# Order of all engines from a plan inside the program; the first gated state turned through DRAM

## The chip, the cores and the metric

The kernel runs on one core of a Trainium2 chip. A core has five engines that run side by side, each with a queue of its own that it works off in order: TensorE (matmuls and transposes into PSUM; PE in the profile, with its weight loads as PEld), VectorE (DVE), ScalarE (ACT), GpSimd (POOL) and SyncE (SP), which issues the DMAs here. The metric is the device time of the whole kernel in microseconds, median of three runs.

## The reference, cut to what matters

128 graphs of 128 nodes with 256 features each; every graph has its own 128x128 adjacency. Four layers, each added to x. Three are graph attention, the last a gated graph network of three steps:

```python
# layers 0, 1, 2 (attention), each with its own W and a
h = relu(layernorm(x))
Wh = h @ W
e = (Wh @ a1)[:, :, None] + (Wh @ a2)[:, None, :]
e = where(e > 0, e, 0.2 * e)
p = softmax(where(adj > 0, e, -9e15), axis=-1)
x = x + elu(p @ Wh)             # layer 2 also multiplies by nodemask
# layer 3 (gated): h = relu(layernorm(x)), then three times, i = 0, 1, 2
m = h @ weight[i]
ag = A.T @ m                    # A = (adj != 0)
r = sigmoid(ag @ w_ih[r].T + h @ w_hh[r].T + b)
z = sigmoid(ag @ w_ih[z].T + h @ w_hh[z].T + b)
n = tanh(ag @ w_ih[n].T + b_in + r * (h @ w_hh[n].T + b_hn))
h = (1 - z) * n + z * h
# out = x + h
```

All of it is in float32.

## The kernel before, in words

Graphs are taken four at a time: 32 groups, 512 columns (4 graphs x 128 nodes) in a PSUM bank. Two Python generators issue the work of a group: `gat(g)` the three attention layers and the start of the gated layer, `gru(g)` the three gated steps.

An attention layer (`attention`, L200) keeps nodes in partitions. `stats` (L170) takes mean and variance on VectorE and the reciprocal deviation rs on GpSimd (L182). ScalarE centres and clips into xn (L207). The two score vectors come from xn without forming Wh: the first on VectorE, one graph at a time (scr, L212), the second as a product pr on GpSimd (L217) that ScalarE scales and sums (L221). Four TensorE transposes (e, L229) turn the second score into a row. VectorE adds, masks and takes the maximum (L235 to L241), ScalarE the exponential (L245), TensorE transposes the probabilities (atp, L261), multiplies by xn (ahp, L272) and by W (hp, L285). ScalarE (L291) and VectorE (L293, L294) form elu and add it to xo, which GpSimd had prepared as x - 1 (L257). The next layer's statistics need xo, so one group's layers are a chain across all engines.

After the third layer the gated state hn (L317) is transposed to feature-major form by `turned` (L185): eight TensorE transposes into two banks (hTp, L191), copied out by ScalarE (L195) and VectorE (L197) into hT.

A gated step (`gru`, L324) works feature-major in two halves of 128 features. Four accumulators stand in four PSUM banks: nn, r, z (from the state and `whh`) and ni, with r, z and ni also fed from the aggregate ag and `wc` (L344; the products weight[i] @ w_ih are formed once in the setup). The state is turned back to node-major by TensorE (hnp, L335), copied by ScalarE (hn, L352), multiplied with the adjacency (agp, L361) and copied by VectorE (ag, L365). wn, r, n, z are activations on ScalarE (L385 to L402), the rest is VectorE (L392 to L408). The last state is turned back once more and added to x (o, L415), and the result is stored (L419).

PSUM's eight banks are split into three rings: two for attention ("gat"), four for the gates ("gru"), two for the turns ("tr"). Tiles come from pools with two buffers for most tags.

Order: the program's end (L428 to L434) issues `gat(0)`, `gat(1)`, then `gru(0)`, `gat(2)`, `gru(1)`, and so on, and the framework's own scheduler interleaves these streams into one order for each engine when the program is built. That order is fixed at run time: an engine whose next instruction waits does nothing else. The setup (weights, their transposes, wc) comes first. VectorE copies its PSUM results.

Of the kernel before, what the change touches and what calls it, by code (L numbers as in the profile page):

```python
# [17 lines left out]
EPS = 1e-5  # L18


@with_exitstack
def kernel(
# [23 lines left out]

    nc = tc.nc
# [3 lines left out]
    NG = B // G  # L51
    T = G * N
    STEPS = gweight.shape[0]
    assert N == P and B % G == 0 and B <= P and D == 2 * P and T == 512

    const = ctx.enter_context(tc.tile_pool(name="const", bufs=1))
    grp = ctx.enter_context(tc.tile_pool(name="grp", bufs=2))
    gw = ctx.enter_context(tc.tile_pool(name="gw", bufs=2))
    setup = ExitStack()
    su = setup.enter_context(tc.tile_pool(name="setup", bufs=2))  # L60
    psum = ctx.enter_context(tc.tile_pool(name="psum", bufs=1, space=bass.MemoryType.PSUM))
    BANKS = {"gat": 2, "gru": 4, "tr": 2}

    def bank(tag, name):
        return psum.tile([P, T], FT, tag=tag, name=name, bufs=BANKS[tag])

    def load(g):
        xt = grp.tile([P, G, D], FT, tag="x0", name=f"x_{g}")
        nc.sync.dma_start(xt, x[g * G : (g + 1) * G].rearrange("b n d -> n b d"))
        at = grp.tile([P, G, N], I32, tag="adj", name=f"adj_{g}")  # L70
        nc.sync.dma_start(at, adj[g * G : (g + 1) * G].rearrange("b i j -> i b j"))
        return xt, at

    loaded = {0: load(0)}


# [4 lines left out]

    W, VA = [], []
    for l, (w, a) in enumerate(((w0, a0), (w1, a1), (w2, a2))):
        wt = const.tile([P, KD, D], FT, name=f"w_{l}")
        nc.sync.dma_start(wt, w.rearrange("(k p) o -> p k o", p=P))
        ab = su.tile([P, 2, D], FT, tag="ab", name=f"ab_{l}")
        nc.sync.dma_start(ab, bass.AP(tensor=a.tensor, offset=a.offset, ap=[[0, P], [1, 2 * D]]))
        wa = su.tile([P, 2, KD], FT, tag="wa", name=f"wa_{l}")  # L90
        vp = bank("gat", f"vp_{l}")
        for s in range(2):
            for k in range(KD):
                scr = su.tile([P, D], FT, tag="scr", name=f"scr_{l}_{k}_{s}")
                nc.vector.scalar_tensor_tensor(
                    scr, wt[:, k, :], 1.0, ab[:, s, :], op0=OP.mult, op1=OP.mult,
                    accum_out=wa[:, s, k : k + 1],
                )
                c = s * KD + k
                nc.tensor.transpose(  # L100
                    vp[:, c * P : (c + 1) * P], wa[:, s, k : k + 1].to_broadcast([P, P]), ident
                )
        va = const.tile([P, 2, D], FT, name=f"va_{l}")
        nc.vector.tensor_copy(va.rearrange("p s d -> p (s d)"), vp)
        W.append(wt)
        VA.append(va)

    nm = su.tile([B, N], FT, tag="nm", name="nm")
    nc.sync.dma_start(nm, nodemask)
    nmp = bank("gat", "nmp")  # L110
    nc.tensor.transpose(nmp[:, :B], nm, ident[:B, :B])
    nmT = const.tile([P, B], FT, name="nmT")
    nc.vector.tensor_copy(nmT, nmp[:, :B])


    def transposed(src, dst, nm_):
        rows = src.shape[0] // P
        t = su.tile([P, rows, D], FT, tag="wld", name=f"{nm_}_ld")
        nc.sync.dma_start(t, src.rearrange("(r p) d -> p r d", p=P))
        for k in range(KD):  # L120
            for r0 in range(0, rows, 4):
                n = min(4, rows - r0)
                ps = bank("gat", f"{nm_}_{k}_{r0}")
                for r in range(n):
                    nc.tensor.transpose(
                        ps[:, r * P : (r + 1) * P], t[:, r0 + r, k * P : (k + 1) * P], ident
                    )
                nc.vector.tensor_copy(dst[:, k, r0 * P : (r0 + n) * P], ps[:, : n * P])
# [341 lines left out]
```

## Time and profile before

| | |
|---|---|
| time | 3127.16 us, median of 3 (3126.57 to 3129.3) |
| span of the profiled execution | 3125.1 us |
| TensorE busy | 2941.1 us, 94% |
| VectorE, ScalarE, GpSimd busy | 2163.8, 1349.4, 530.0 us |
| DMA | 48.03 MB, mean 15 GB/s |
| first gate product nn | at 121.09 us |
| stores of neighbouring results, middle groups | 94.27 us apart |

A busy row adds the times of an engine's instructions. Idle time in front of an instruction is put down to what released it last. Matmul ends are modelled and overlap their successors, so the distance of two starts says more of a matmul's cost than its printed length. A float32 matmul stands as two passes in the records, a transpose as one.

### The profile page before, as it was taken

Reading aid. Unit: us, or ns where it says so; the run is one execution under the profiler, and the core shown is the slowest. Engines: PE = TensorE matmul, PEld = TensorE weight load, DVE = VectorE, ACT = ScalarE, POOL = GpSimd, SP = SyncE. Lnnn points to the kernel's source line nnn. Section 1 sums busy time; section 2 is a strip of 40 time slices with the busy share of each in tenths; the row PEclk is TensorE's granted clock in tenths of the full one; section 3 lists DMA queues with packets and bytes.
Section 4 is the critical chain, followed back from the end, with each engine's and each line's share of the span. In section 5 each row is a group of like instructions: output and inputs, shape, how many; then the busy total and the mean of one; then the engine's idle time right before and its main releaser. Section 6 shows DMA issues by size and latency. Waiting matters only on the chain.

```text
span 3125.1 us, 32601 instructions
## 1 busy us (share of the span) xinstructions
PE 2941.1 (94%) x11105; PEld 1714.3 (55%) x11105; DVE 2163.8 (69%) x4731; ACT 1349.4 (43%) x3265; POOL 530.0 (17%) x454
## 2 busy tenths in 40 slices
PE   5699999999999999999999999999999999999999
PEld 3455555555555555555555555555555555555554
DVE  5667776767776777776777677677667677767663
ACT  1344444444444444444444444444444444444442
POOL 1212111212111212121112121112121121111110
PEclk8899999999999999999999999999999999999999
DMA  2000000000000000000000000000000000000000
GB/s 85 11 17 11 7 18 17 17 18 11 7 18 17 18 17 11 7 17 18 17 18 11 7 17 18 18 12 13 11 18 17 17 11 7 17 14 7 8 1 14
DMA packets 56199, 48.03 MB, mean 15 GB/s; under 512 B 3296, under 2 KB 55648, under 8 KB 56032
## 3 DMA queue, kind: packets, MB, share of 16 engines
q1 hardware_dynamic: 56032, 45.95, 4.6%
q8 instruction: 87, 1.43, 0.2%
q14 instruction: 80, 0.66, 0.1%
HBM read 29.17 MB, written 16.78 MB: 15 GB/s over the span
## 4 chain that ended last, share of the span: by engine, by line
PE 70%; DVE 13%; ACT 9%; POOL 6%; issue 1%; DMA 0%; ACTq 0%; SPq 0%; POOLq 0%; DVEq 0%
PE r L344 15%; PE z L344 15%; PE ni L344 9%; PE hp L285 7%; PE nn L344 7%; PE ahp L272 6%; POOL pr L217 5%; ACT xn L207 4%; PE agp L361 3%; DVE st L175 3%; DVE xo L294 3%; DVE xo L293 3%; ACT pr L221 2%; PE hnp L335 2%; PE e L229 2%; PE atp L261 2%
## 5 line engine op out<-in xcount | busy, mean ns | idle before, releaser
L212 DVE SCALAR_TENSOR_TENSOR scr<-xn,rs,va 128x256 f32<-128x256 f32 x384 | 386.0, 1053 | 73.0 <-POOL rs L182 71.1
L344 PE MATMUL r<-ag,wc 128*128 128x512 f32 x768 | 372.1, 593 | 0.0
L344 PE MATMUL ni<-ag,wc 128*128 128x512 f32 x768 | 371.4, 592 | 0.0
L285 PE MATMUL hp<-w,ah 128*128 128x256 f32 x1536 | 368.3, 383 | 0.7 <-DVE ah L279 0.7
L344 PE MATMUL z<-ag,wc 128*128 128x512 f32 x768 | 361.4, 592 | 0.0
L257 POOL TENSOR_SCALAR xo<-xo 128x1024 f32<-128x1024 f32 x64 | 67.5, 1055 | 1596.4 <-DVE mv L176 1596.4
L285 PEld LDWEIGHTS hp<-w,ah 128*128 128x128 f32 x1536 | 284.2, 190 | 76.8 <-DVE ah L279 26.3
L293 DVE SCALAR_TENSOR_TENSOR xo<-hp,xo 128x512 f32<-128x512 f32 x192 | 131.0, 683 | 253.6 <-ACT t L291 253.6
L221 ACT ACTIVATE pr<-pr,rs 128x256 f32<-128x256 f32 x384 | 190.4, 496 | 183.5 <-POOL pr L217 183.5
L291 ACT ACTIVATE t<-hp 128x512 f32<-128x512 f32 x192 | 114.7, 597 | 353.5 <-PE hp L285 353.5
L344 PE MATMUL nn<-h,whh 128*128 128x512 f32 x512 | 261.8, 593 | 0.0
L344 PE MATMUL z<-h,whh 128*128 128x512 f32 x512 | 261.5, 592 | 0.0
L344 PE MATMUL r<-h,whh 128*128 128x512 f32 x512 | 261.5, 592 | 0.0
L392 DVE SCALAR_TENSOR_TENSOR n<-r,wn 128x512 f32<-128x512 f32 x192 | 131.4, 685 | 185.2 <-ACT r L390 185.2
L217 POOL TENSOR_TENSOR pr<-xn,va 128x1024 f32<-128x1024 f32 x96 | 236.2, 2461 | 96.6 <-ACT xn L207 96.6
L245 ACT ACTIVATE pe<-em,nmx 128x128 f32<-128x128 f32 x384 | 148.8, 389 | 209.3 <-DVE nmx L241 209.3
L361 PEld LDWEIGHTS agp<-am,hn 128*128 128x128 f32 x1536 | 204.5, 192 | 61.3 <-issue 61.0
L344 PEld LDWEIGHTS z<-ag,wc 128*128 128x128 f32 x768 | 143.3, 190 | 167.5 <-issue 167.4
L397 ACT ACTIVATE n<-n,bi 128x512 f32<-128x512 f32 x192 | 138.3, 720 | 213.1 <-DVE n L396 210.5
L390 ACT ACTIVATE r<-r,brz 128x512 f32<-128x512 f32 x192 | 131.3, 684 | 215.1 <-PE r L344 215.0
L344 PEld LDWEIGHTS ni<-ag,wc 128*128 128x128 f32 x768 | 143.5, 190 | 142.7 <-issue 132.2
L361 PE MATMUL agp<-am,hn 128*128 128x128 f32 x1536 | 218.2, 275 | 0.0
(91 smaller groups left out, 4636.6 us busy)
## 6 DMA issues: line engine op xcount, KB each, us to landing
x<-in_x_dram SPq DMA_DIRECT2D x32, 512.0 KB, 3.9
out_dram<-o SPq DMA_DIRECT2D x32, 512.0 KB, 2.9
adj<-in_adj_dram SPq DMA_DIRECT2D x32, 256.0 KB, 2.7
w<-in_L_gnn_W_dram SPq DMA_DIRECT2D x3, 256.0 KB, 6.9
ab<-in_L_gnn_a_dram SPq DMA_DIRECT2D x3, 256.0 KB, 6.6
whh_ld<-in_L_gnn_w_hh_dram SPq DMA_DIRECT2D x1, 768.0 KB, 8.4
wih_ld<-in_L_gnn_w_ih_dram SPq DMA_DIRECT2D x1, 768.0 KB, 5.9
gt_ld<-in_L_gnn_weight_dram SPq DMA_DIRECT2D x3, 256.0 KB, 2.6
```

The costliest lines, as they stand in the source:

```text
L212: nc.vector.scalar_tensor_tensor(scr, xn[:, b, :], rs[:, b : b + 1], VA[l][:, 0, :], op0=OP.mult, op1=OP.mult, accum_out=e[:, 0, b : b + 1],)
L217: nc.gpsimd.tensor_tensor(pr, xn, VA[l][:, 1 : 2, :].to_broadcast([P, G, D]), op=OP.mult)
L221: nc.scalar.activation(pr[:, b, :], pr[:, b, :], AF.Copy, scale=rs[:, b : b + 1], accum_out=e[:, 1, b : b + 1],)
L245: nc.scalar.activation(pe[:, b, :], em[:, b, :], AF.Exp, bias=nmx[:, b : b + 1], accum_out=sm[:, b : b + 1])
L272: nc.tensor.matmul(ps[:, c * P : (c + 1) * P], xn[:, c, k * P : (k + 1) * P], at[:, c * P : (c + 1) * P], start=True, stop=True,)
L285: nc.tensor.matmul(hp[:, b * D : (b + 1) * D], ah[:, k, c * P : (c + 1) * P], W[l][:, k, :], start=(k == 0), stop=(k == KD - 1),)
L293: nc.vector.scalar_tensor_tensor(u, hp, 0.0, u, op0=OP.max, op1=OP.add)
L344: nc.tensor.matmul(ps, w[:, k, c * P : (c + 1) * P], v[k], start=start, stop=stop)
L361: nc.tensor.matmul(ps[:, b * P : (b + 1) * P], hn[k][b], am[:, b, :], start=True, stop=True)
L390: nc.scalar.activation(r, pr, AF.Tanh, bias=brz[:, cr : cr + 1], scale=0.5)
L392: nc.vector.scalar_tensor_tensor(n, r, 1.0, wn, op0=OP.add, op1=OP.mult)
L397: nc.scalar.activation(n, n, AF.Tanh, bias=bi[:, cn : cn + 1])
```

## The change

The kernel's arithmetic stays. What changes is who sets the order, and how the first gated state is turned.

1. A plan in the program. No instruction is issued directly any more. Each is handed to `plan.add` with its engine, an estimated cost, a rank and the values that it reads and writes. `Plan.issue` then plays the program through with these costs: at each step it takes the engine that can start earliest, and of its instructions that could start within 0.1 us of the first the one of lowest rank. An instruction may run ahead of the lowest unfinished rank by at most 6. The list that comes out is issued with the framework's scheduler switched off (`manual_schedule`), so it is each engine's order.
2. Tiles by first use. A value takes its buffer in a ring when its first instruction is placed, so the order of buffers follows the plan; `takes` makes the first instruction of a chain claim what the rest needs.
3. Ranks. Group g's gated step i has 3g + i, its attention layer l has 3g - 7.5 + 2l. The layers of a group lie thus over the gated steps of groups up to two earlier, and two groups' layers overlap. ScalarE's and VectorE's gate work is put forward by 2 (URGENT).
4. Groups. The first and the last have two graphs, the 31 between them four.
5. The first gated state. VectorE transposes 32x32 blocks of hn into tr, one DMA stores tr to DRAM, four load it back with the blocks exchanged (hT). Its blocks lie so that the first gated step reads the state with a strided view (`first`): runs of 32 values. The eight TensorE transposes and two copies of `turned` are gone.
6. Small moves: setup copies go from VectorE to ScalarE; the exponential and the normalised probabilities are written in place of the scores (em); GpSimd's xo comes ahead of the score transposes in the program; gate products are ranked rather than listed.

The core of the diff:

```diff
+class Plan:
+    LAG = {"PE": 0.26, "DVE": 0.08, "ACT": 0.08, "POOL": 0.12, "SP": 2.4}
+    WINDOW = 0.1
+    AHEAD = 6.0
...
+        def choose(engine):
+            found = [(start(op), op) for op in ready[engine]]
+            found = [f for f in found if f[0] is not None]
+            if not found:
+                return None
+            first = min(t for t, _ in found)
+            soon = [(op.rank, t, i) for i, (t, op) in enumerate(found) if t <= first + self.WINDOW]
+            _, t, i = min(soon)
+            return t, found[i][1]
...
+        for op in order:
+            for v in op.vals:
+                v.t
+            op.fn()
...
-    NG = B // G
+    SIZES = [2] + [G] * ((B - 4) // G) + [2]
+    NG = len(SIZES)
...
+    def dve(cols):
+        return 0.1 + cols / 960
+
+    def act(cols):
+        return 0.25 + cols / 1400
+
+    def pool(cols):
+        return 0.35 + cols / 512
...
+        rank = 3.0 * g - LEAD + 2.0 * l
...
-        hT = turned(hn, grp, "h0", f"{g}_3")
...
+        def blocks(k):
+            add("DVE", dve(n * P), rank, lambda: nc.vector.transpose(
+                tr.t[:, :, :F].rearrange("p j (k b c) -> p k b j c", k=KD, b=n)[:, k],
+                hn.t[:, :, k * P : (k + 1) * P].rearrange("p b (j r) -> p b j r", j=Q),
+            ), reads=[hn], writes=[(tr, k)])
...
+        add("SP", 0.45, rank, lambda: nc.sync.dma_start(
+            d.t.rearrange("q r j f -> (q r) j f"), tr.t[:, :, :F]), reads=[tr], writes=[d])
+
+        def back(j):
+            add("SP", 0.45, rank, lambda: nc.sync.dma_start(
+                hT.t[j * 32 : (j + 1) * 32, :, :F], d.t[:, :, j, :].rearrange("q r f -> r q f")
+            ), reads=[d], writes=[(hT, j)])
...
+        def first(k):
+
+            t = h0.t[:, :, :F].rearrange("p q (k b c) -> p k b q c", k=KD, b=n_g)
+            return t[:, k]
...
-    AHEAD = 2
-    for g in range(min(AHEAD, NG)):
-        run(gat(g))
-    for g in range(NG):
-        run(gru(g))
-        if g + AHEAD < NG:
-            run(gat(g + AHEAD))
+    LEAD, URGENT = 7.5, 2.0
+    for g in range(NG):
+        gru(g, *gat(g))
+    with tc.manual_schedule():
+        plan.issue()
```

## The prediction

> **What bounds the kernel now.** I read the busy shares first, then TensorE's own waits, then one steady wait and the start in the time-ordered view.
>
> ```profile
> PE 2941.1 (94%) x11105; PEld 1714.3 (55%) x11105; DVE 2163.8 (69%) x4731; ACT 1349.4 (43%) x3265; POOL 530.0 (17%) x454
> ...
> PE   5699999999999999999999999999999999999999
> ...
> PEclk8899999999999999999999999999999999999999
> ```
>
> TensorE is busy in 94% of the span and no other engine comes near. The three missing tenths lie in the first two or three slices; after that every slice shows a 9, which can hide up to a tenth. So time can come from three places: less TensorE work, a shorter start, or the few per cent hidden inside the nines. The second view gives busy time by stretch (columns: stretch, its length, busy PE, PEld, DVE, ACT, POOL, granted clock, DMA share, GB/s):
>
> ```profile
> 0.00:40.00 40.00, 23.32 (x82) 14.18 (x83) 25.00 (x79) 5.07 (x13) 6.51 (x11) 1.00 0.55 166
> 40.00:80.00 40.00, 18.81 (x71) 13.31 (x71) 20.51 (x45) 8.85 (x31) 5.76 (x5) 0.71 0.00 0
> 80.00:120.00 40.00, 18.48 (x74) 13.79 (x73) 20.97 (x58) 11.36 (x31) 7.18 (x8) 0.67 0.02 7
> 240.00:1240.00 1000.00, 959.21 (x3656) 560.43 (x3655) 711.15 (x1557) 448.64 (x1089) 177.77 (x151) 1.00 0.04 14
> ```
>
> In the first 120 us TensorE works 60.6 us, part of it at a clock of 0.7. In steady state 40.8 us of every 1000 are idle. TensorE's waits say for whom (total us, times, longest):
>
> ```profile
> PE e L229 <- ACT pr L221: 102.4, 125, 8.4
> PE hTp L191 <- ACT hn L317: 29.1, 33, 6.1
> PE atp L261 <- DVE pe L252: 16.6, 3, 5.8
> PE vp L100 <- DVE scr L95: 14.3, 2, 9.6
> PE e L229 <- DVE scr L212: 8.5, 1, 8.5
> ```
>
> The last three and the longest of the others belong to the start (events of 5 to 10 us). What remains is one habit: four small transposes of a score column, e (L229), and eight of the gated state, hTp (L191), stand in TensorE's queue earlier than their inputs. In the queue that looks so:
>
> ```profile
> 1561.88 1.02 PE L344 MATMUL r<-ag,wc 128*128 128x512 f32 x2
> 1564.04 0.32 PE L229 MATMUL e<-ident,e 128*128 128x128 f32 x1 [1.14 <-ACT pr L221]
> 1564.53 0.32 PE L229 MATMUL e<-ident,e 128*128 128x128 f32 x1 [0.17 <-ACT pr L221]
> 1564.69 1.02 PE L344 MATMUL r<-ag,wc 128*128 128x512 f32 x2
> ```
>
> A ready gate product stands behind an unready transpose. That is order, not lack of work.
>
> **Work per group.** Starts of neighbours give the cost, since the printed ends overlap. Four 512-column passes start 1.72 us apart (1501.44 to 1503.16), so 0.430 each. In the same way 256 columns cost 0.216, 128 columns 0.111 and a transpose 0.109. One group of four graphs has 144 gate passes (61.9 us), 48 + 48 passes of agp and ahp (10.7), 48 of hp (10.4), 56 transposes (6.1): 89.0 us. In the time-ordered view the results' stores of middle groups start 94.27 us apart (1448.22 to 1542.49). The loss is 5.3 us a group: 3.8 recorded as idle (107.7 of the 2700 us from 240 to 2940), the rest about 0.2 of refill after each of several waits, as in the two short steps above.
>
> [...] scr (L212) has a median of 482 ns and a maximum of 2639, beside GpSimd's pr of 2447. A plan without that lock is late by some 2.0 us a layer. [...] no run here shows TensorE with a strided input. [...]
>
> **The change, part by part.**
>
> *Transposes of the first gated state.* Removed per group: eight on TensorE (8 x 0.109 = 0.87 us), a ScalarE copy (0.56), a VectorE copy (0.68). Added: two VectorE block transposes of 512 columns, 0.69 each from the other 512-column rows (bounds 0.5 to 1.4 us), one store and four loads of 512 KB together in each direction. The page shows 2.9 us for a store and 3.9 for a load of that size; DMA is at 4 to 5% and will be near 10%. On the path to the first gate product (nn) this takes about 7.5 us instead of some 2, but the distance in TensorE's new order between the group's last hp and its nn is 81 us of work (24 before). Hidden, except in the first groups. VectorE's sum grows by 32 x (1.4 - 0.7) = 22 us and loses about 16 of setup copies to ScalarE: under 76% of the new span.
>
> *Strided input.* The first of three steps now reads its moving operand in runs of 32 values. That concerns 24 passes a group, 24 x 0.43 x 32 = 330 us. I take no extra cost (runs of 128 bytes); the other end is one and a quarter to double.
>
> *The order.* I took both programs' instruction order on TensorE and summed the work above between producer and consumer, for the middle groups (median us; "need" is what the chain takes on an idle machine, from the gaps at the start of before):
>
> | from, to | need | before | after |
> |---|---|---|---|
> | hp to next layer's e | 8.5 | 8.6 | 39.7 |
> | hp to hTp | 6.1 | 5.8 | gone |
> | e to atp | 5.4 | 6.9 | 10.3 |
> | atp to ahp | 0.8 | 1.7 | 1.7 |
> | ahp to hp | 0.9 | 0.9 | 0.9 |
> | hnp to agp, second half | 0.9 | 7.8 | 0.9 |
> | agp to gate product, second half | 1.0 | 1.3 | 2.6 |
>
> The first two rows are the two waits: before, the distance equals the need on an idle machine, and any queue on ScalarE or GpSimd turns into idle TensorE. After, it is more than four times the need, because two groups' layers alternate. The new tight place is agp behind hnp (twice a group): hnp's end to ScalarE's copy 0.2, copy 0.59, wake-up 0.1, 0.9 in all against 0.86 of gate work between. ScalarE's preceding instruction, wn, ends before, so I take 0.05 us each. The lock falls on scr; queued behind it are the gate's n operations, and TensorE's ring of four banks needs them 7.3 us after agp, while the queue needs about 5.9 with the lock. It fits with 1.4 us to spare. I take 0.4 us a group for all residues (bounds 0 and 3): 31 x 0.4 = 12 us.
>
> *Start.* The first group has two graphs, setup lies between its layers, and the second group's layers run beside it. Its first e needs weights landed (about 7 us), scores' weights and copy (to 12), products (to 15.5). A layer on two graphs, from the trace's gaps with per-graph parts halved: e to atp 3.5, to ahp 1.0, ahp 2, hp 2.5, to the next e 6.7: 15.7 us where the trace shows 24. The third layer's hp ends near 56; then statistics, normalising, block transposes and two DMA landings of 3 us make nn start at 70 (121 before). From there to the second group's nn are 54.7 us of TensorE work, with some 5 to 8 of waits since half-size chains are not covered: 131 us, at which 97.9 us of work are done. Loss 33 us; before it was 80 at its first nn (40.6 us of work done by 121.1) and 9 more by the second (97.6 us for 88.5 of work).
>
> *End.* Two graphs alone: 35.1 us of work, about 5 us of waits, and 4 for the last store.
>
> **Sum.** Work: 31 x 88.1 + 2 x 44.1 for the half groups + 21 for setup = 2840. Plus start 33, residues 12, end 9: 2894; I take 2898, leaving 4 us for low clock in the start. The same sum for before, from its own times: 121 to the first nn, 98 to the second, 30 x 94.3, then 70 of work and 8 to the end: 3126, as measured. The gain of some 229 us is made of 147 us of waits in the middle groups (30 x 5.3 - 12), 28 of work that is gone (2868 - 2840) and 56 in the start (80 + 9 - 33).
>
> **Rivals.** (a) The waits come back elsewhere: every tight place carries a share of the lock and of wrong durations in the plan, 2 to 3.5 us a group, half of what is lost now: 2898 + 31 x 2.5 = 2975. For it: 0.9 against 0.9 at agp, and a static order can't yield. Against: ahp to hp stood at 0.9 before and cost 0.7 us in the whole run. (b) The strided read costs a quarter: 2898 + 82 = 2980. (c) It costs double, or more: 2898 + 330 = 3228, slower than before. For it: nothing in the trace shows such a read. [...]
>
> **How the numbers follow.** Forecast 0.72, (a) 0.18, (b) 0.06, (c) 0.04. Low end 2868: no residues, a start as short as its chain, no waits at the end. High end 2972 takes in nearly all of (a). Faster: the first three, 0.95; within 0.2% 0.01; slower 0.04.
>
> **What would show it.** Right: e waits on ScalarE gone from TensorE's list outside the start; PE at 98 to 99% in the steady stretches; results' stores 88.1 to 89 us apart; nn of the second group near 131 us. Wrong: agp waiting on ScalarE's hn or gate products on VectorE's ag or n for over 1 us a group (a); first-step gate passes starting more than 0.43 apart (b, c); nn waiting on DMA after the first groups. What would break the forecast most is a queue of VectorE that falls behind its plan by more than the 1.4 us, since every group would then repeat it.

## The result, and the profile after

The changed kernel takes 2987.74 us (median of 4 runs, 2986.42 to 2988.23), the kernel before in the same comparison 3126.93: a ratio of 0.9553, 95% interval 0.9536 to 0.9569. It is faster, by 139 us where 229 were forecast, and lies 16 us above the range. The page of the changed kernel:

```profile
PE 2914.3 (98%) x10993; PEld 1703.4 (57%) x10993; DVE 2131.0 (71%) x4800; ACT 1351.7 (45%) x3294; POOL 510.2 (17%) x468
...
PE   6789999999999999999999999999999999999998
```

TensorE has risen from 94% to 98%, and the start still shows 6, 7 and 8. The same stretches as before, and some of TensorE's waits over the whole run:

```profile
0.00:40.00 40.00, 21.43 (x89) 15.10 (x90) 18.81 (x72) 16.17 (x44) 8.43 (x14) 0.91 0.57 170
40.00:80.00 40.00, 26.75 (x109) 17.58 (x107) 29.24 (x74) 16.91 (x52) 13.55 (x14) 0.87 0.02 7
80.00:120.00 40.00, 28.30 (x131) 23.16 (x132) 30.01 (x79) 18.70 (x60) 10.18 (x9) 0.79 0.09 27
240.00:1240.00 1000.00, 997.60 (x3739) 574.99 (x3738) 735.43 (x1644) 464.84 (x1131) 178.01 (x158) 1.00 0.08 27
```

```profile
...
PE e L467 <- DVE em L473: 8.1, 6, 3.9
PE e L467 <- ACT pr L444: 6.3, 4, 3.5
PE ahp L528 <- DVE at L516: 5.6, 4, 3.3
```

The waits of the old order are gone: e waits for ScalarE four times (6.3 us) instead of 125 times (102.4), all in the start, and hTp does not exist any more. Where 40.8 us of 1000 were idle in the steady part, 2.4 are. By this view nothing should be left to lose there. Yet the stores of middle groups come 89.5 us apart (485.32 to 2723.39 over 25 groups; distances of stores below are medians), 1.4 more than the work.

To place the difference I went along TensorE's order of each kernel, summed the work at the prediction's prices (0.430, here unrounded as 0.4295, 0.216, 0.111, 0.109), and took that sum from the time at which the trace has the instruction. What is over is loss (nn is a group's first gate product):

| at | time | work before it | loss | loss forecast |
|---|---|---|---|---|
| first group's nn | 101.4 | 43.2 | 58.2 | 27 |
| second group's nn | 173.4 | 97.9 | 75.5 | 33 |
| third group's nn | 283.3 | 190.8 | 92.5 | 37 |
| last group's nn | 2940.9 | 2805.6 | 135.3 | 49 |
| end | 2986.2 | 2840.6 | 145.6 | 58 |

(The forecast's 4 us for low clock are in the third line.) So of the 88 us by which this execution exceeds 2898, 56 lie in the start (to the third group), 31 in the 30 groups of the steady part (1.43 us a group instead of 0.4) and 1 at the end.

### The profile page after: what moved, and what is told of

The parts are those of the page before. It is cut to its first block, busy times and chain, and to the rows that moved or that the text cites. A ratio compares the mean times of both kernels' runs of the same rounds, so it can differ in the third digit from the quotient of the medians.

```text
span 2986.2 us, 32859 instructions
## 1 busy us (share of the span) xinstructions
PE 2914.3 (98%) x10993; PEld 1703.4 (57%) x10993; DVE 2131.0 (71%) x4800; ACT 1351.7 (45%) x3294; POOL 510.2 (17%) x468
## 4 chain that ended last, share of the span: by engine, by line
PE 93%; DVE 4%; ACT 1%; issue 1%; DMA 0%; POOL 0%; SPq 0%; ACTq 0%; DVEq 0%
PE r L685 22%; PE z L685 21%; PE hp L551 11%; PE nn L685 11%; PE ni L685 11%; PE ahp L528 6%; PE agp L707 6%; PE hnp L664 3%; PE e L467 1%; PE atp L510 1%; DVE scr L438 1%; DVE xo L569 1%; DVE xo L567 1%; DVE h L774 0%; DVE st L405 0%
## 5 line engine op out<-in xcount | busy, mean ns | idle before, releaser
L685 PE MATMUL nn<-h,whh 128*128 128x512 f32 (+1 forms) x792 | 396.1, 582 | 3.4 <-DVE h L774 3.4
L685 PE MATMUL z<-h,whh 128*128 128x512 f32 (+1 forms) x792 | 397.3, 583 | 0.2 <-DVE n L750 0.2
L685 PE MATMUL r<-h,whh 128*128 128x512 f32 (+1 forms) x792 | 396.2, 582 | 0.4 <-ACT r L742 0.4
L685 PE MATMUL r<-ag,wc 128*128 128x512 f32 (+1 forms) x792 | 395.4, 581 | 0.9 <-DVE ag L715 0.9
L685 PE MATMUL z<-ag,wc 128*128 128x512 f32 (+1 forms) x792 | 395.3, 581 | 0.0
L685 PE MATMUL ni<-ag,wc 128*128 128x512 f32 (+1 forms) x792 | 394.4, 580 | 0.0
L565 ACT ACTIVATE t<-hp 128x512 f32<-128x512 f32 x192 | 107.5, 595 | 348.4 <-DVE xo L567 344.9
L453 POOL TENSOR_TENSOR pr<-xn,va 128x1024 f32<-128x1024 f32 (+1 forms) x99 | 235.4, 2378 | 127.9 <-ACT xn L431 122.5
L685 PEld LDWEIGHTS r<-h,whh 128*128 128x128 f32 x792 | 150.5, 191 | 165.1 <-issue 141.1
L491 ACT ACTIVATE em<-em,nmx 128x128 f32<-128x128 f32 x384 | 149.4, 390 | 182.1 <-DVE nmx L487 181.9
L528 PEld LDWEIGHTS ahp<-at,xn 128*128 128x128 f32 x1536 | 183.1, 195 | 75.7 <-DVE at L516 72.0
```

The source lines that it names most:

```text
L453: add("POOL", pool(n * D), rank, lambda: nc.gpsimd.tensor_tensor(pr.t, xn.t, VA[l].t[:, 1:2, :].to_broadcast([P, n, D]), op=OP.mult), read ...
L491: add("ACT", 0.58, rank, lambda: nc.scalar.activation(em.t[:, b, :], em.t[:, b, :], AF.Exp, bias=nmx.t[:, b : b + 1], accum_out=sm.t[:, b ...
L528: add("PE", pe(P), rank, lambda: nc.tensor.matmul(ps.t[:, b * P : (b + 1) * P], xn.t[:, b, k * P : (k + 1) * P], at.t[:, b, :], start=True ...
L565: add("ACT", act(T), rank, lambda: nc.scalar.activation(t.t, hp.t, AF.Exp), reads=[hp], writes=[t])
L685: nc.tensor.matmul(o, w.t[:, k, c * P : (c + 1) * P], m, start=start, stop=stop)
```

## The experiments

All kernels, with the loss up to the third group's nn ("start") and the loss per group from there to the last group's nn ("steady"), in the same measure. "Handovers" are the times that the plan allows between the end of an instruction and the start of one that needs it on another engine (LAG); the "hold" (the prediction's "lock") is the time by which an instruction of VectorE takes longer beside one of GpSimd: in the changed kernel up to 2.68 us for scr instead of 0.48. Times are medians, ratios against the kernel before with their intervals.

| kernel | time | ratio | start | steady |
|---|---|---|---|---|
| changed | 2987.7 | 0.9553 (0.9536 to 0.9569) | 92.5 | 1.43 |
| e1, turn on TensorE | 3030.2 | 0.9684 (0.9670 to 0.9699) | 92.9 | 1.91 |
| e2, before with DRAM turn | 3121.0 | 0.9974 (0.9963 to 0.9985) | | |
| e3, larger handovers | 3004.3 | 0.9598 (0.9584 to 0.9612) | 76.7 | 2.54 |
| e4, pr cut | 2957.2 | 0.9451 (0.9437 to 0.9465) | 72.9 | 1.06 |
| e5, larger handovers and pr cut | 2913.8 | 0.9317 (0.9303 to 0.9331) | 58.3 | 0.13 |
| e6, hold in the plan | 2956.2 | 0.9452 (0.9436 to 0.9467) | 70.4 | 1.12 |
| e7, hold in the plan, handovers | 2937.7 | 0.9394 (0.9380 to 0.9408) | 58.5 | 0.89 |
| e8, LEAD 6 | 3045.2 | 0.9738 (0.9724 to 0.9753) | 79.0 | 3.77 |
| e9, e7 and setup later | 2950.1 | 0.9425 (0.9411 to 0.9439) | 64.4 | 1.14 |
| e10, e7 and LEAD 6 | 3029.4 | 0.9678 (0.9664 to 0.9693) | 60.8 | 3.88 |
| e11, e7 and freed buffers | 3068.2 | 0.9797 (0.9781 to 0.9814) | 66.2 | 5.10 |
| e12, second score on VectorE, handovers | 2922.0 | 0.9342 (0.9328 to 0.9356) | 64.3 | 0.21 |
| e13, e7 with pr in pieces | 2921.6 | 0.9341 (0.9326 to 0.9357) | 62.3 | 0.27 |
| e14, first group alone | 3005.5 (one run) | | 117.1 | |
| e15, turn at the bank | 2988.6 | 0.9553 (0.9539 to 0.9567) | 79.8 | 1.88 |
| e16, hold and turn | 2954.3 | 0.9444 (0.9428 to 0.9460) | 61.4 | 1.33 |
| e18, all in one | 2921.4 | 0.9337 (0.9323 to 0.9351) | 64.9 | 0.13 |

One reservation holds for e6, e7, e9 to e11, e13 to e16 and e18: with the hold or the turn in it, the plan meets two engines that could start at the same time, and which comes first depends on how Python lists a set. Building e7, e13 and e15 anew gave two different orders each; the changed kernel, e3 and e12 gave one. What another order is worth in time was not measured; differences of some us among those kernels are therefore no finding.

### The turn through DRAM, taken out and put in alone (e1, e2)

```diff
 # e1, on the changed kernel
-        for k in range(KD):
-            blocks(k)
...
+        for k in range(KD):
+            turn(k)     # 4 tensor.transpose into a "gat" bank, copied out by ScalarE / VectorE
...
-                        o, m = cut(ps.t[:, :TG]), first(k)
+                        o, m = ps.t[:, :TG], first(k)
 # e2, on the kernel before: the same exchange the other way round
```

> The changed kernel with its part 5 undone: TensorE turns the first gated state (eight transposes a group) and the first step reads it in whole rows; the plan stays. My theory: the DRAM turn saves TensorE 0.87 us in each of 32 groups, and nothing of it lies on a path in the steady part, so this run is 28 us slower than the changed kernel: about 3015 us, stores about 0.9 us further apart (90.4). The start should not change much, since nn of the first groups would come 3 to 5 us earlier with a turn on TensorE. Rival: the trip through DRAM or the strided read costs elsewhere what it saves on TensorE; then this run takes the same time as the changed kernel, 2988, or less.

> The kernel before with only the first gated state turned by VectorE and DRAM; order by the framework's scheduler as before. My theory: 0.87 us of TensorE work and 0.9 us of waits at hTp go, per group, 32 times, so about 57 us less: 3065 to 3075. Rival: in the old order only 24 us of work lie between hp and the first gate product, so the work saved comes back as a wait of the first gate products for the loads, or as longer waits at e; then 3110 to 3130.

e1 took 3030.2 us, 42 more than the changed kernel, where 28 were expected: 0.88 us a group of work (89.0 instead of 88.1) and 0.48 of loss. Its list of waits has the second part; the kernel before had 29.1 us there:

```profile
PE hTp L617 <- ACT t L565: 18.2, 30, 1.0
```

So the turn through DRAM is worth more than its work, and costs nothing that is seen in the steady part. In the start it delays the first group (nn at 101.4 instead of 89.3), but by the third group both have lost the same (92.5 and 92.9).

e2 went the rival's way: 3121.0, 8 us under the kernel before. The stores come 93.5 us apart instead of 94.27, which is less than the 0.87 us of removed work alone, and the first group's nn comes at 141.6 instead of 121.1. The hTp wait is gone and others have taken its place (e had 102.4 before):

```profile
PE e L235 <- ACT pr L227: 110.4, 129, 8.5
...
PE z L354 <- DVE n L407: 18.1, 29, 0.7
```

So in the old order the steady part gains the 0.8 us a group of saved work, some 24 us in all, and no wait besides; the start, where nn comes 20 us later, gives most of it back. Why it comes so much later was not followed up. The same edit is worth 8 us in the old order and some 42 in the new; everything else without it gains 99 (3129.3, the kernel before in the same comparison, to 3030.2). The parts of this change do not add.

The strided read has no cost. Starts of first-step products in the changed kernel, two passes a line:

```profile
292.32 1.02 PE L685 MATMUL nn<-h,whh 128*128 128x512 f32 x2
...
293.18 1.02 PE L685 MATMUL r<-h,whh 128*128 128x512 f32 x2
...
294.04 1.02 PE L685 MATMUL z<-h,whh 128*128 128x512 f32 x2
```

0.86 us for two passes, 0.430 each. All 744 strided passes of 512 columns have a median distance of 0.429 us to the next start, as have the 1488 in whole rows. Rivals (b) and (c) are out.

### Handovers and the hold (e3, e4, e5)

After the result I had two suspects for the loss of 1.43 us a group. The first does not show as idle TensorE but in front of its weight loads, from 283 to 2900 us:

```profile
PEld agp L707 <- ACT hn L696: 75.1, 115, 0.7
PEld ahp L528 <- DVE at L516: 65.0, 86, 0.8
PEld hp L551 <- DVE ah L539: 44.3, 85, 0.7
```

These sums are not the loss: they come to 184 us, and from the third group's nn to the last's only 43 are lost, so most of the waiting lay beside an earlier product that still ran. But with no slack the first load shows. One case in the time-ordered view of the changed kernel:

```profile
502.34 0.60 PE L664 MATMUL hnp<-ident,h 128*128 128x128 f32 x4
...
502.78 1.02 PE L685 MATMUL z<-h,whh 128*128 128x512 f32 x2
...
502.98 0.58 ACT L696 COPY hn<-hnp 128x512 f32<-128x512 f32 x1 [1.10 <-PE hnp L664]
503.62 0.97 PEld L707 LDWEIGHTS agp<-am,hn 128*128 128x128 f32 x8 [0.64 <-ACT hn L696]
503.64 1.14 PE L707 MATMUL agp<-am,hn 128*128 128x128 f32 x8
...
504.61 0.60 PE L685 MATMUL r<-ag,wc 128*128 128x512 f32 x1
```

z ends its 0.86 us at 503.64, and in that moment hn is ready: no idle time is recorded. But the eight agp passes take 0.97 instead of 0.89. Summed over 600 to 2600 us (22.3 groups), start-to-start times exceed the prices by 8.8 us at agp, 7.5 at ahp and 5.5 at hp: 0.10, 0.11 and 0.08 for each of the four, three and three such places of a group, 1.0 us a group together. A further 6 us lie at r, 2 each at z and nn.

The second suspect is the hold that the prediction named, of VectorE by GpSimd's pr. Here two instructions of the changed kernel in its start:

```profile
74.08 2.63 POOL L453 TENSOR_TENSOR pr<-xn,va 128x1024 f32<-128x1024 f32 x1 [2.12 <-ACT xn L431]
...
74.43 2.56 DVE L438 SCALAR_TENSOR_TENSOR scr<-xn,rs,va 128x256 f32<-128x256 f32 x1
```

scr, 0.48 us in the median, takes 2.56 here: pr started 0.35 us before it and took 2.63, and scr ended 0.28 us after pr's end (76.99 and 76.71).

```diff
 # e3
-    LAG = {"PE": 0.26, "DVE": 0.08, "ACT": 0.08, "POOL": 0.12, "SP": 2.4}
+    LAG = {"PE": 0.36, "DVE": 0.28, "ACT": 0.28, "POOL": 0.32, "SP": 2.4}
 # e4
-            pr.t, xn.t, VA[l].t[:, 1:2, :].to_broadcast([P, n, D]), op=OP.mult
+            pr.t[:, :, 0:1], xn.t[:, :, 0:1], VA[l].t[:, 1:2, 0:1].to_broadcast([P, n, 1]), op=OP.mult
...
-                pr.t[:, b, :], pr.t[:, b, :], AF.Copy, scale=rs.t[:, b : b + 1],
+                pr.t[:, b, :], xn.t[:, b, :], AF.Copy, scale=rs.t[:, b : b + 1],
 # e5: both
```

e4 and e5 leave out the multiplication with the second score vector: they show what the hold costs, and their result is not the reference's.

> The changed kernel with larger handover times in its plan (LAG: TensorE 0.36, VectorE and ScalarE 0.28, GpSimd 0.32), so that TensorE places ahp, agp and hp later behind their inputs: the second half's agp gets 1.7 us of work between instead of 0.9, ahp to hp 1.2 instead of 0.9. Theory: the loss of 1.43 us a group in the steady part comes from inputs that arrive just in time, with weight loads exposed that do not count as idle; then the stores come 88.5 to 88.7 us apart instead of 89.5 and the time falls by 25 us to about 2960. Rival: the loss has nothing to do with the handovers (the passes themselves cost more, or VectorE's queue is late); then the time stays within 5 us of 2988.

> The changed kernel with GpSimd's product pr cut to one column of each graph; ScalarE sums xn in its place, so the multiplication with the second score vector is left out and the second score is not the reference's. The order of the engines is nearly the same. Takes away the overlap in which GpSimd's 2.4 us instruction holds VectorE. Theory: the start is bound by VectorE's queue, of which the hold is a part (some eight layers with up to 2 us each before the third group's first gate product); then nn of the third group comes 10 to 20 us before 283 and the steady loss falls a little (below 1.2 us a group): 2960 to 2975. Rival: the hold falls beside other work everywhere; then nn of the third group stays within 3 us of 283 and the time within 5 us of 2988.

> The larger handover times of the third experiment together with the cut product of the fourth (the multiplication with the second score vector is left out). In the third the waits at agp and ahp went but TensorE's z waited 2.15 us a group for ScalarE's z and VectorE's n, whose queue had stood behind an xo that GpSimd's pr held back. Theory: handovers and the hold are the two halves of the loss, so with both away the stores come 88.3 to 88.8 us apart (89.5 in the changed kernel, 90.85 and 89.1 in the two alone), and the time is 2930 to 2945. Rival: the z wait comes from the bank order that the larger handover times produce; then it stays and the stores remain near 90.5, time near 2980.

e3 was slower, 3004.3, against both of its expectations. Its mechanism held: agp's weight loads wait 0.7 us in all instead of 75.1, and the start became 16 us shorter. But the stores stand 90.85 apart, since TensorE's z now waits 39.4 us for ScalarE's z and 20.5 for VectorE's n. The view in order of time gives the chain:

```profile
732.48 3.43 DVE L569 SCALAR_TENSOR_TENSOR xo<-t,xo 128x512 f32<-128x512 f32 x2
...
732.89 2.48 POOL L453 TENSOR_TENSOR pr<-xn,va 128x1024 f32<-128x1024 f32 x1 [3.22 <-ACT xn L431]
...
739.07 1.16 POOL L459 TENSOR_SCALAR xo<-x 128x1024 f32<-128x1024 f32 x1
...
739.25 0.99 DVE L606 TENSOR_TENSOR nm<-nm,rs 128x4 f32<-128x4 f32 x1
...
740.27 0.60 ACT L610 ACTIVATE hn<-xo,nm,rs 128x256 f32<-128x256 f32 x1 [2.03 <-DVE nm L606]
740.77 0.67 ACT L757 ACTIVATE z<-z,brz 128x512 f32<-128x512 f32 x1
...
741.50 1.12 PE L685 MATMUL z<-h,whh 128*128 128x512 f32 x2 [1.47 <-ACT z L757]
```

Two xo of 0.69 us take 3.43, because pr starts before the second. VectorE's queue is late; nm, a matter of 0.16 us, is held once more by GpSimd's own xo (0.99); ScalarE's hn waits 2.03 us for nm; z, whose input has long been there, stands behind hn; and TensorE needs the bank that z reads. Four engines pass these holds on.

e4 fits its theory, though the time is 3 us below the range: 2957.2, start 20 us shorter, steady 1.06. VectorE's busy time falls by 135 us (2131.0 to 1996.2) for the same number of instructions, and the longest scr from 2676 to 1285 ns (the changed kernel, then e4):

```profile
L438 DVE SCALAR_TENSOR_TENSOR scr<-xn,rs,va x384: 470/482/2676, 13.9 to 2826.3; 128x256 f32<-128x256 f32 x192
```

```profile
L438 DVE SCALAR_TENSOR_TENSOR scr<-xn,rs,va x384: 473/481/1285, 14.5 to 2795.6; 128x256 f32<-128x256 f32 x192
```

e5 is 2913.8, below what was expected, and settles the steady part. Its stores:

```profile
448.73 0.38 SPq L796 DMA_DIRECT2D out_dram<-o  x1
...
536.89 0.38 SPq L796 DMA_DIRECT2D out_dram<-o  x1
...
625.05 0.38 SPq L796 DMA_DIRECT2D out_dram<-o  x1
```

88.16 apart, for 88.1 of work, and from 600 to 2600 us agp, ahp and hp lose 0.4 us together where they lost 21.8. In the start the two act side by side: handovers alone 15.8 us, the hold alone 19.6, both 34.2. In the steady part they do not: +1.1, -0.4, and together -1.3 a group. In e3's order the hold falls on xo and costs more than the handovers gain, so they pay only once it is away.

### With all work done: the hold in the plan (e6, e7), LEAD, setup, freed buffers (e8 to e11)

```diff
 # e6: GpSimd's pr and xo, VectorE's scr, both em on em, xo<-t, n<-r, all of d and h get lock=True
+            if op.lock:
+                t = max(t, *held_till.values())
...
+            if op.lock:
+                held_till[e] = op.end
 # e7: e6 with the LAG of e3
 # e8: LEAD 7.5 -> 6.0   # e9: e7, SETUP -3.0 -> -1.6   # e10: e7, LEAD 6.0
 # e11: e7, and in lag():
-        return 0.0 if d.engine == engine else self.LAG[d.engine] if data else 0.08
+        return 0.0 if d.engine == engine else self.LAG[d.engine] if data else 0.28
```

> The changed kernel with the hold known to the plan: [...] nothing else is altered and all work is done. Theory: the hold made VectorE late against its plan; a plan that knows it puts other work beside pr, so most of what the fourth experiment gained comes without leaving work out: start 10 to 20 us shorter, stores 89.1 to 89.3 apart, 2960 to 2970. Rival: VectorE is so full in the start that no order helps, and the hold only moves to other instructions: 2980 to 2995.

> The hold known to the plan and the larger handover times, all work done. Theory: both causes of the loss treated: stores 88.4 to 88.9 us apart, 2940 to 2955, a version that beats both kernels. Rival: a static order with the hold in it leaves z waiting as in the third experiment, stores 89.5 to 91 apart, 2985 to 3010.

> The changed kernel with LEAD 6.0 in place of 7.5: the attention layers of later groups are ranked half a group later against the gated steps, so fewer of them stand in the start beside the first groups' chains. Theory: the start is long because VectorE has to do layers of four groups before the third group's first gate product; with fewer ahead the start is 10 to 25 us shorter, the steady distance stays within 0.3 us of 89.5: 2960 to 2980. Rival: the start is bound by the first group's own chain of dependent instructions (TensorE is half idle from 60 to 100 us whatever the other groups do), or by a lack of other work for TensorE; then the start stays or grows: 2985 to 3010.

> The seventh experiment's kernel (hold in the plan, larger handover times) with the setup ranked behind the first group's layers (SETUP -1.6 instead of -3), all work done. Asks for the rest of the start, which still loses 58 us at the third group's first gate product where the prediction had 34. Theory: from 20 to 57 us the setup's products and copies stand between the first group's layers, and from 57 to 90 TensorE lacks work; with the setup behind, the first group's chain runs ahead: its first gate product at 78 to 85 instead of 89.6 us, time 2925 to 2932. Rival: the first group's chain is held by VectorE's and ScalarE's other work, not by the setup; then the first gate product stays within 3 us of 89.6 and the time within 5 of 2938.

> The seventh experiment's kernel with LEAD 6. In the eighth, LEAD 6 alone shortened the start by 13.5 us and cost 2.3 us a group in the steady part. Theory: that steady cost is again the hold and the handovers, met at other places; with both in the plan it goes to about what the seventh has (88.9) and the shorter start stays: 2922 to 2932. Rival: the layers then stand too close behind one another for the chain whatever the plan knows, stores stay over 90 apart: 2975 or more.

> The seventh experiment's kernel, in which e still waits 0.5 us a group for VectorE's em to leave its PSUM bank, with the plan's handover for a freed buffer raised from 0.08 to 0.28 us. Theory: the plan undervalued that kind of handover too: the e waits go, stores 88.4 to 88.7 us apart instead of 88.92, 2925 to 2932. Rival: the 0.8 us left are VectorE's lateness from durations that the plan has wrong, and e waits as before: within 4 us of 2938.

Of VectorE's instructions that e6 locks, the trace of the changed kernel shows five held: scr, xo<-t, n<-r, h and the first em took up to 2.68, 2.72, 2.53, 2.73 and 1.36 us, in the median 0.48 and four times 0.68 to 0.69. The others, the second em and d, stayed at 0.69; that they too can be held was the author's assumption.

e6 and e7 went the way of their theories and came 2 to 4 us below their ranges, at 2956.2 and 2937.7 (stores 89.17 and 88.92 apart): a plan that knows the hold gains as much as leaving pr out (2957.2), and the larger handovers now help. But e6 was to keep the held instructions apart, and on the chip it does not:

```profile
L445 DVE SCALAR_TENSOR_TENSOR scr<-xn,rs,va x384: 462/481/2643, 14.4 to 2794.9; 128x256 f32<-128x256 f32 x192
```

From 600 to 2600 us scr takes 112 us more in all than undisturbed (the lowest twentieth of its durations), and 112 in the changed kernel. In the steady part the gain of e6 comes from an order that reckons with the hold, not from fewer or shorter holds.

e8 was half right: the start loses 13.5 us less, inside what was expected, but the steady part loses 2.3 us a group more, and the time goes up by 57. e10 did not mend that. Its agp waits 57.3 us in 31 cases for ScalarE's hn; one of them in order of time:

```profile
921.43 1.11 POOL L466 TENSOR_SCALAR xo<-x 128x1024 f32<-128x1024 f32 x1
921.56 1.52 DVE L752 SCALAR_TENSOR_TENSOR n<-r,wn 128x512 f32<-128x512 f32 x1
...
922.27 0.60 PE L671 MATMUL hnp<-ident,h 128*128 128x128 f32 x4
922.71 0.38 PE L474 MATMUL e<-ident,e 128*128 128x128 f32 x2
...
923.90 0.72 ACT L759 ACTIVATE n<-n,bi 128x512 f32<-128x512 f32 x1 [1.42 <-DVE n L757]
...
924.53 0.56 ACT L703 COPY hn<-hnp 128x512 f32<-128x512 f32 x1
...
925.15 1.16 PE L714 MATMUL agp<-am,hn 128*128 128x128 f32 x8 [2.06 <-ACT hn L703]
```

Only two transposes stand between hnp and agp: the ranks offered TensorE nothing else at this place. And hn is late because it stands on ScalarE behind an n that waits 1.42 us for VectorE, whose own n takes 1.52 us instead of 0.69 beside GpSimd's xo. The trace has that long n, in each case beside an xo of GpSimd, once in every group from 275 to 2580 us. So the hold has a part in this too, though the plan knows of it; how much of the 2.06 us is its share was not taken apart. e9 missed as well: the first group's nn came at 94.2, where 78 to 85 was expected, and the time grew by 12 us, so its rival missed too.

e11 was the worst, against both of its expectations. Every second group its e waits 3.0 to 3.7 us and its agp 2.8. Two lines show where it begins:

```profile
1016.27 3.44 DVE L576 SCALAR_TENSOR_TENSOR xo<-t,xo 128x512 f32<-128x512 f32 x2
...
1016.50 2.66 POOL L460 TENSOR_TENSOR pr<-xn,va 128x1024 f32<-128x1024 f32 x1 [2.90 <-ACT xn L438]
```

The plan had placed these apart. On the chip they met, since the plan fixes the order on each engine, not between the two. VectorE's em behind it came late, and with it e. The other cases begin in the same way: from 450 us on, each of the 13 long waits of e has one xo of 2.8 us, beside pr, 8 to 9 us before it. Why the new handover time brings the two together was not followed up.

### The length of the hold (e12, e13)

```diff
 # e12, with the LAG of e3: pr on GpSimd and its sums on ScalarE are replaced by
+            add("DVE", dve(D) + 0.08, rank, lambda: nc.vector.scalar_tensor_tensor(
+                pr.t[:, b, :], xn.t[:, b, :], rs.t[:, b : b + 1], VA[l].t[:, 1, :], op0=OP.mult,
+                op1=OP.mult, accum_out=e.t[:, 1, b : b + 1],
+            ), reads=[(xn, b), rs, VA[l]], writes=[(pr, b), (e, (1, b))])
 # e13, on e7: pr in four instructions
+        def weighed(b):
+            add("POOL", 0.1 + D / 440, rank, lambda: nc.gpsimd.tensor_tensor(
+                pr.t[:, b, :], xn.t[:, b, :], VA[l].t[:, 1, :], op=OP.mult
+            ), reads=[(xn, b), VA[l]], writes=[(pr, b)], lock=True)
```

> The changed kernel with the larger handover times and the second score formed on VectorE, as the first one is (four instructions of 0.41 us a layer in place of GpSimd's pr of 2.4 us and ScalarE's sums), all work done. Takes away the long hold without leaving work out. Theory: the hold is the main cause, its loss on VectorE (135 us between the changed kernel and the one with the cut product) nearly pays for the 384 new instructions (157 us), so stores come 88.2 to 88.6 us apart and the start loses 55 to 65 us: 2913 to 2930, a version that beats all before. Rival: VectorE, at some 74%, is then the engine that is late: stores 89 to 91 apart, 2940 to 2990.

> The seventh experiment's kernel with pr as four instructions of one graph each on GpSimd in place of one of four graphs, all work done. The sum of the hold stays, its longest piece falls from 2.4 to about 0.7 us. Theory: what hurts is the length of one hold at a place where VectorE's queue has no slack, since everything queued behind waits; so stores come 88.3 to 88.7 us apart (88.92) and the start gets shorter by some us: 2918 to 2932. Rival: it is the sum of the hold that counts: 2935 to 2945, or more if each piece costs GpSimd a fixed time.

Both came where the theory had them, and within 1 us of one another: 2922.0 and 2921.6, versions that do all the work and beat both kernels, the changed one by 2.2%. Only e13's start is not shorter than e7's, as it should have been: it loses 62.3 us, e7's 58.5. In e12 VectorE does more (2152.5 us, 74%), in e13 GpSimd does (580.9 instead of 510.2, a piece takes 731 ns). The sum of the hold has hardly fallen in e13: from 600 to 2600 us VectorE's instructions take 71 us more than undisturbed, in e7 82. The longest piece has, from 2.2 us of hold to 0.8; in e7 it lies on xo. That instruction in e7 and in e13:

```profile
L576 DVE SCALAR_TENSOR_TENSOR xo<-t,xo x192: 679/682/2847, 31.5 to 2823.0; 128x512 f32<-128x512 f32 x192
```

```profile
L580 DVE SCALAR_TENSOR_TENSOR xo<-t,xo x192: 677/683/1222, 36.9 to 2808.4; 128x512 f32<-128x512 f32 x192
```

This speaks for the length of single holds, and not their sum, as what hurts. Other traces agree: e5 and e12 lose next to nothing though GpSimd's xo holds nm by 0.8 us in every group, and e16 (below) has a sum of only 34 us, in holds of up to 1.8 us, and loses no less than e6 with 115. But two rivals stand, which e13 does not separate from the length. Its pieces also fall elsewhere, 41 of the 71 us on scr, and e6, with holds of 2.1 us there, loses hardly more than e4 without pr's hold (1.12 and 1.06). And with four pieces ScalarE's sums need not wait for the whole of pr.

### The rest of the start (e14)

```diff
 # e14, on e7: cap and the first layer's st of every group g > 0
+            after=behind       # the store of the first group's tr
```

> The seventh experiment's kernel with the attention layers of all other groups kept back until the first group's gated state is turned, all work done; it is meant to be slower, and only its first group is looked at. Theory: a layer of two graphs takes 15.7 us when nothing stands beside it, as the prediction had it, first gate product at 70 to 75 us, so that the rest of the start's error is the other groups' work in front of the first group's (VectorE and ScalarE are taken in turns); in the seventh experiment the layers take 18.2 and 19.4 us and the first gate product comes at 89.6. Rival: the chain by itself is longer than I took it: first gate product at 82 us or later.

Neither came true. The first group's chain with no other group beside it, e of the three layers and nn:

```profile
20.36 0.27 PE L474 MATMUL e<-ident,e 128*128 128x128 f32 x1
...
38.42 0.27 PE L474 MATMUL e<-ident,e 128*128 128x128 f32 x1
...
54.40 0.47 PE L474 MATMUL e<-ident,e 128*128 128x128 f32 x1 [6.52 <-ACT pr L451]
...
79.18 1.19 PE L694 MATMUL nn<-h,whh 128*128 128x256 f32 x2 [6.68 <-DMA h<-d]
```

The first e comes 4.9 us after my 15.5; the layers take 18.0 and 16.0 where I had 15.7; from the last e to nn it is 24.8 where I had 23. Together that is 79.2 instead of 70. The other groups' work adds 10.4 (89.6 in e7). Keeping it back is no gain: the loss at the third group is then 117 us instead of 58.

### The turn at the bank (e15, e16), and all together (e18)

ScalarE's t and VectorE's xo read the same bank, hp. In the trace of the changed kernel t waits 344.9 us for xo and xo 77.3 for t, and the plan does not know of it. I took this for the reason why hn is late in front of agp.

```diff
 # e15
-                reads=[hp], writes=[t])
+                reads=[hp], writes=[t], turn=hp)     # and so for xo: one reader at a time
 # e16: e15 and e6          # e18: e15 and e13
```

> The changed kernel with one more thing known to its plan: ScalarE's t and VectorE's xo both read the bank hp, and the trace shows them taking turns (t waits 345 us in all for xo, xo 77 us for t), while the plan lets them read at once. Nothing else is altered; TensorE's steady order stays the same. Theory: t comes late, ScalarE's hn stands behind it, and agp's weight load waits for hn (75 us, 115 times); with the turn in the plan those waits go, the loss falls by the agp part (about 0.4 us a group) or more: stores 88.8 to 89.2 us apart, 2965 to 2978. Rival: hn is late for another reason (durations, wake-up): stores stay within 0.15 of 89.53, time within 6 of 2988.

> The changed kernel with the hold and the turn at the bank known to its plan, handover times as in the changed kernel, all work done; TensorE's steady order is again the same. Theory: hold, turn and handovers are separate parts of the loss; against the hold alone (89.17 apart, 2956) the turn takes 0.4 us a group or more: 88.6 to 88.9 apart, 2938 to 2948. Rival: no difference to the hold alone, 2950 to 2960.

> All in one, all work done: hold and turn in the plan, larger handover times, pr in four pieces. Theory: steady part at its floor, stores 88.1 to 88.4 us apart, start no longer than the thirteenth experiment's: 2905 to 2922. Rival: the parts no longer add once little is left and a new order costs something elsewhere: 2922 to 2950.

That theory fell. t no longer waits for xo, but agp's weight loads wait as before, 72.8 us in 115 cases, and the time is the same (2988.6; 13 us won in the start, given back in the steady part):

```profile
PEld agp L714 <- ACT hn L703: 72.8, 115, 0.6
```

In the half of a step where hn had stood behind t, it now comes earlier, but the plan, which sees this too, has moved agp up by one product. Both halves then look like the case shown above: from the end of hnp to agp's first weight load the chain takes 0.86 us (502.78 to 503.64), and the plan puts 0.86 us of work between (608.51 to 609.37 in e15). The plan fills the slack it sees; in these runs only the larger handover times made it leave some (agp's 0.7 us in e3). That also undoes the part of the expectation which had TensorE's order unchanged. e16 adds nothing to e6 that can be measured (2954.3 and 2956.2, with ratios whose intervals overlap). e18 reaches the floor in the steady part (88.15 apart) and loses 64.9 us in the start, 2921.4 in all: no better than e12 and e13.

## Why the prediction was wrong

The direction was right and so were most steps; two terms of the sum were far too small: the residues of the steady part (12 us taken, 43 measured) and the loss of the start (37 taken, 92.5 measured).

- *What bounds the kernel, and the two waits.* Right. Both waits of the old order are gone; 2.4 us of 1000 are idle instead of 40.8.
- *Work per group, 88.1.* Right to a tenth: 88.16, 88.16 and 88.15 in e5, e12 and e18.
- *The turn through DRAM.* Right in kind: 28 us of work, 42 with the wait that it takes along (e1), hidden but for the first group. As an edit of its own it is nearly worthless (e2).
- *Strided input at no cost.* Right: 0.430 a pass. The forecast's zero was the author's estimate; no run before it showed such a read.
- *End.* 45.3 us after the last group's first nn, where I had 44.1.
- *Residues, "0.05 us each", "0.4 us a group for all".* Wrong: 1.43 a group, 43 us instead of 12. The table had the tight places in it, atp to ahp, ahp to hp, hnp to agp, with the distance equal or nearly equal to the need, and I priced only agp, twice a group. There are ten such places in a group, and each costs 0.08 to 0.11 us of exposed weight load with no idle time recorded: 1.0 us. That ahp to hp "cost 0.7 us in the whole run" before was read from the list of idle waits, which does not show this cost.
- *The lock, "it fits with 1.4 us to spare".* Right in the place, wrong in the price. The hold does fall on scr: 112 of the 114 us by which VectorE's instructions from 600 to 2600 us take longer than undisturbed. And n bears it: in the steady part TensorE waits for it once, 0.2 us. But I asked only for that wait and put nothing more, and the hold costs some 0.4 us a group (1.43 against 1.06 in e4), mostly as delayed starts of r. That it falls on scr was luck of this order: in e3 it meets xo and costs as much as 2.2.
- *Start, loss 33 and 4 for low clock.* Wrong: 92.5. The hold and the handovers make 34 us of the difference (e5 loses 58.3). The other 21 lie before the first group's nn, which comes at 91.1 in e5 instead of 70; from there to the third group e5 loses 10, as forecast. Of the 21, the first group's chain was 9 us too short as I priced it (e14, one run), and 10 us are what the other groups' work takes from it, which I had left out (89.6 in e7 against 79.2 in e14). The 2 us that remain were not taken apart.
- *Rivals.* (a) has nearly the right time, 2975, for the wrong reason: it put 2 to 3.5 us a group of waits into the steady part, where 1.43 are lost, and nothing more into the start.

Behind the larger part of the residues stands the reading that a distance equal to the need costs nothing, since no idle time is recorded. Behind the hold's part, in the steady part and the start, stands another: I took the plan's order as carried out. The plan's numbers said that VectorE would be on time. The trace of before held the evidence that it would not be, a scr of 2639 ns, and I used it for one chain instead of asking for every queue what 2 us of delay would do to it.

## What to carry to other kernels

When an order is computed ahead, list every place where an input arrives just when it is needed, and price each (here 0.1 us) even where the profile records no idle time; compare start-to-start times with undisturbed ones to see it. A hold of one engine by another that the plan does not know is best put into it: with one hold of 2.4 us 0.89 us a group were lost then, and 2.54 where the plan did not know of it (e7 and e3). It is worth a trial to make its single holds short as well: in pieces of 0.7 us 0.27 were lost (e13). Putting it into the plan does not keep the two apart on the chip (e6, e10, e11): the plan orders each engine, not one against the other. And judge such a change with both measures apart, start and steady part: settings that shortened the one (LEAD 6, larger handovers) lengthened the other.

## What the runs showed of the hardware

- Inputs of TensorE that arrive just in time cost time that is not recorded as idle: the changed kernel has 0.2 us of idle TensorE from 600 to 2600 us and loses 30. With larger handovers and without the hold (e5) it loses less than 1 there. The waits stand in the weight-load rows (75.1 us for agp, 0.7 in e3), and what they cost only in the distances of starts (0.97 us for eight agp passes instead of 0.89).
- GpSimd's smaller instructions hold VectorE too: its xo of 1.16 us made VectorE's nm take 0.99 us instead of 0.16 (e3; in the changed kernel nm starts 0.05 us before xo, at 475.89, and takes 0.165), and one of 1.11 us made n take 1.52 instead of 0.69 (e10).
- TensorE read its moving operand in runs of 32 values of float32 as fast as in whole rows (0.430 us for 512 columns).
